# A two-layer adaptive graph network on one core: Strassen's scheme for one more softmax stage, and row statistics, norm parts and weights at other places in the written-out order

## The chip, the cores and the metric

The kernel runs on one core of one Trainium2 chip. The metric is the device time of one execution in microseconds (us), smaller is better. Times of several executions of a kernel are compared by their median. All arithmetic on TensorE is float32.

## The reference

Two layers of the same form follow each other; each is an adaptive graph convolution with a residual connection and a layer norm. With N = 2048 nodes, B = 8 batches, C = 64 features and an embedding of D = 16 numbers a node:

```
layer 0:  supports I, A, 2 A A - I
layer 1:  supports I, A, 2 A A - I, S     S = softmax(relu(E E^T), axis=1)
x_g = einsum("knm,bmc->bnkc", supports, x)
w   = einsum("nd,dkio->nkio", E, weights_pool)      weights of each node
out = einsum("bnki,nkio->bno", x_g, w) + E @ bias_pool
x   = layernorm(x + out)
```

A is 2048 x 2048. So for every node block the kernel needs u = A x, then A u, in layer 1 also S x, and for every node its own 64 x 64 weights for each support.

## The kernel before

**Stages.** The work is cut into 40 stages, listed as `stages` (line 744): five phases of eight node blocks of 256 nodes each, stage n = 8 i + j. Phase A0 makes u = A x of layer 0, B0 makes A u and closes layer 0 with the norm, A1 makes u = A x of layer 1, Z1 makes S x, V1 makes A u of layer 1 and closes with the norm. So stages 16 to 23 are A1, 24 to 31 are Z1, and 32 to 39 are V1. x and u (2048 x 512) stay on chip.

**The products.** Each stage has a generator `product` that yields its matmuls one by one. A plain stage (`straight`, or `turned`) multiplies directly: in `turned` the features are held as the stationary side in 128 columns and the adjacency or softmax block of 256 nodes is streamed, which makes 64 matmuls of 128x256 into accumulators called pz. The other stages use Strassen's scheme with its Winograd sums (`strassen`, line 471): seven products (p1, p4, p7, p2, p6, p5, p3 in this order) of half-size quarters, and additions on VectorE (DVE) with temporaries (`temps`) afterwards, which also write the results to u or to the turned features t. In phases B0 and V1 the quarters and sums of A come ready from HBM; in A0 four quarters are streamed and their sums are made in place by `sum_of_a`.

**Softmax stages.** Numerators are exp(relu(E E^T) - c), c being the row maximum (S is needed transposed, E E^T is symmetric, so c and the reciprocal of the row sum are laid along the streamed nodes and broadcast over the partitions by `load_e`, which also loads the embedding of the block into e, two buffers `e2` in turn). In stages 24 and 25 `scores` makes two slices of 128 rows at a time: two matmuls (ps), one scalar_tensor_tensor on DVE (p<-ps,c 128x512) and one exponential on ScalarE (ACT), into four buffers of tag `f2k`; the division by the row sum happens on the way from pz to t (`turned_half`). From stage 26 the blocks are taken in pairs, "wide": `numerators` makes four slices at a time (128x1024) into quarters in `w_room`, the room of the node weights, which is free then; `normalize` multiplies a quarter (128x2048) by the row's reciprocal sum, and Strassen's scheme runs over two blocks, 7 products of 32 matmuls of 256 columns in stages n and n+1 together.

**Row statistics.** In A1, `scores_of_rows` makes rows of E E^T (pr) and their maximum, `statistics` the exponentials with their row sums on ACT, and `store_c` writes both to HBM for Z1.

**Other jobs of a stage.** `weights` (line 319) makes the weights of a block: groups of matmuls pw<-e,wst into the three large PSUM buffers (`ps_big`, two banks each), whose contents go to w by ACT and, every third one, by DVE; `turn` transposes x or u through PSUM (pt) and copies it to t, half by DVE and half by ACT; `apply` multiplies the features of each node by its weights (po) and adds the 4x4 diagonal blocks to acc on DVE with a mask; `post` is the layer norm in parts 0 (mean, subtraction, squares on ACT), 1 (variance, square root on ACT) and 2 (reciprocal, product, store). The large PSUM buffers serve pw, pt, ps, pr, pb and po alike. Two accumulators (`ps_acc`) serve the products.

**Order.** All engines keep the order in which the program issues their instructions (`Pinned`, line 33; this is why nearly every profile line says L43). That order is written by hand: `put(n, place, job)` and `spread` lay jobs at places 0 to 64 of stage n (scaled by the stage's `length`), and the main loop calls `catch_up` after each matmul, which issues the jobs whose place is reached. Weights of stage n are made in stage n+1 for phases A0, B0 and A1, except for the last block of B0. The adjacency comes through the queue `adj`, an `Ahead` of four stream buffers "a" (128x1024): a load is issued as soon as a buffer can be had in the order of the list `adj.order`.

```
def put(n, i, f, *args):
    plans[n].setdefault(i * stages[n].length / 64, []).append((f, args))
```

Of the kernel before, what the change touches and what calls it, by code (L numbers as in the profile page):

```python
# [48 lines left out]
def two_graph_layers(ctx: ExitStack, tc: tile.TileContext, x, x_t, adj_b, adj_q, layers, out):  # L49
# [167 lines left out]
        for q in range(4):  # L217
            pool.dma_start(out=s1[q * D:(q + 1) * D, :].bitcast(F32), in_=estk[1][(q // 2) * D:(q // 2 + 1) * D, :])

    plain = {("A0", 0), ("A0", 1), ("B0", 0), ("A1", 0)}  # L220

    factors = {1: (("quarter", (0, 0)), "A11", "B11"), 2: (("quarter", (0, 1)), "A12", "B21"), 3: (("sum", 3), "A12", "B22"),
               4: (("quarter", (1, 1)), "A22", "T4"), 5: (("sum", 0), "A21", "T1"), 6: (("sum", 1), "A22", "T2"),
# [22 lines left out]
    def load_adj(t, key):  # L246
# [6 lines left out]
        else:  # L253
# [2 lines left out]

    quarters = [("quarter", at) for at in ((0, 0), (1, 1), (1, 0), (0, 1))]
    adj = Ahead(4, lambda: stream.tile([P, 4 * NB], F32, tag="a", name="a"), load_adj,
                [key for phase in ("A0", "B0", "A1", "V1") for j in range(NBLK)
                 for key in ([("plain", j, i) for i in range(NJ // 4)] if (phase, j) in plain  # L260
                             else [(kind, j, i) for kind, i in (quarters if phase == "A0" else
                                                           [factors[p][0] for p in orders.get((phase, j), usual)])])])
    wst = Ahead(3, lambda: three.tile([P, 8, P], F32R, tag="wst", name="wst"),
                lambda t, kc: sp.dma_start(out=t.bitcast(F32), in_=wd[kc[0]][kc[1]]),
                [(k, c) for k in ((0, 0), (0, 1), (1, 0), (1, 1)) for _ in range(NBLK)
# [2 lines left out]
    class Stage:  # L268
        def __init__(self, n, phase, j):
            self.n, self.phase, self.j = n, phase, j  # L270
            self.li, self.kk = int(phase[1]), int(phase[0] != "A")
            self.half = phase == "B0"
            self.plain = (phase, j) in plain
            self.wide = phase == "Z1" and j >= 2
            self.length = 64 if self.plain or phase == "Z1" and j < 2 else 56
            self.units = C // 2 if self.half else C
            self.e2 = e2[n % 2]
            self.t = self.sq = None
            self.dev = {}


        def load_e(self):
            cols = slice(self.j * NB, (self.j + 1) * NB)
            for h in range(2):
                pool.dma_start(out=self.e2[64 * h:64 * h + 64, :].bitcast(F32), in_=estk[self.li][:, cols])
            if self.phase == "Z1":
                self.c = (one.tile([P, 2, NB], F32, tag="wsplit", name="c") if self.j == 1
                          else two.tile([P, 2, NB], F32, tag="c", name="c"))
                pool.dma_start(out=self.c, in_=cd[self.j].rearrange("k s p -> k (s p)").partition_broadcast(P))

# [130 lines left out]
        def product(self):  # L421
            if self.wide:
                if self.j % 2 == 0:
                    self.rest = self.pair[1].rest = self.strassen(X)
                    return islice(self.rest, self.length)
                return self.rest
            if self.phase == "Z1":
                return self.turned(X, self.softmax())
            if self.kk:
                return self.turned(U, self.loaded()) if self.plain else self.strassen(U)  # L430
            if self.n == 0 or (self.phase, self.j) == ("A0", NBLK - 1):
                self.slabs = U[SB * self.j:SB * self.j + SB]
            else:
                made = one.tile([P, SB, BC], F32, tag="wraw", name="u")
                self.slabs = [made[:, s, :] for s in range(SB)]
            return self.straight(X) if self.plain else self.strassen(X)
# [34 lines left out]
        def strassen(self, right):  # L471
# [8 lines left out]
            if self.wide:  # L480
                temps = [four.tile([P, BC], F32, tag="f2k", name="temp") for _ in range(3)]
                mine = {f"A{h + 1}{t + 1}": self.pair[h].quarters[t] for h in range(2) for t in range(2)}
            else:
                room = one.tile([P, 4, half], F32, tag="wsplit", name="temps")
                temps = [room[:, i, :] for i in range(4)]
                mine = {}
            nodes = NB if self.wide else P
            streamed = self.phase == "A0"
            inside = streamed or self.wide

            def quarter(name):
                if streamed:
# [24 lines left out]
            def add(dst, a, b, op=ALU.add):  # L517

                if not isinstance(dst, tuple):
                    dve.tensor_tensor(dst, a, b, op=op)  # L520
                elif self.kk == 0:
                    dve.tensor_tensor(self.slabs[dst[0]][:, dst[1] * half:(dst[1] + 1) * half], a, b, op=op)
                else:
                    if self.wide:
                        to = self.pair[dst[0]].features()[64:128, :, :]
                    else:
                        to = self.features()[0:64, dst[0] * P:(dst[0] + 1) * P, :]
                    for par in range(2):
                        of = lambda x: x[64 * par:64 * par + 64, :].rearrange("p (q n) -> p n q", n=nodes)
                        dve.tensor_tensor(to[:, :, 4 * dst[1] + par:4 * dst[1] + par + 3:2], of(a), of(b), op=op)  # L530
# [58 lines left out]
        def repeat(self, s):  # L589

            if self.wide:
                self.pair[s].store_z()
            if self.half:
                t = self.t[:, s * P:(s + 1) * P, :]
                if self.j == NBLK - 1:
                    act.copy(t[64:128, :, :], t[0:64, :, :])
                else:
                    pool.dma_start(out=t[64:128, :, :], in_=t[0:64, :, :])
# [64 lines left out]
        def numerators(self, t, part):  # L663

            ps = big("ps").rearrange("p a (m n) -> p (a m) n", n=NB)
            for i in range(4):
                m = 2 * (4 * part + i) + t
                pe.matmul(ps[:, i, :], s1[:, m * P:(m + 1) * P], self.e2, start=True, stop=True)
            p = self.quarters[t][:, part * 1024:(part + 1) * 1024]
            dve.scalar_tensor_tensor(p.rearrange("p (m n) -> p m n", n=NB), ps, 0.0,  # L670
                                     self.c[:, 0, None, :].to_broadcast([P, 4, NB]), op0=ALU.max, op1=ALU.subtract)
            act.activation(p, p, AF.Exp)

        def normalize(self, t):
            p = self.quarters[t].rearrange("p (m n) -> p m n", n=NB)
            dve.tensor_tensor(p, p, self.c[:, 1, None, :].to_broadcast([P, NJ // 2, NB]), op=ALU.mult)

# [117 lines left out]
    for n, st in enumerate(stages):  # L795
# [12 lines left out]
        elif phase == "B0":  # L808
            for c in range(NJ // 4 if st.j == 0 else 0):
                put(n, (10, 26, 36, 57)[c], st.sums_of_a, c)  # L810
            if st.j == 7:
                spread(n, 38, 54, weights)
                bursts, posts = (0, 0, 6, 10), ()
                put(n + 1, 16, st.load_x, range(SB))
                for k in range(6):
# [3 lines left out]
                bursts, posts = (19, 19, 29, 29), (38, 46.5, 50)  # L819
                put(n + 2, 5, st.load_x, range(SB))  # L820
        elif phase == "A1":
            spread(n + 1, 12, 34.5, weights)
            turned, bursts, posts = 4, (43, 43, 43, 43), (56,)
            for s, h, place in ((0, 0, 38), (0, 1, 40), (1, 0, 57), (1, 1, 60)):
                put(*((n, place) if st.j or s == 0 else (n + 1, place - 43)), st.scores_of_rows, s, h)
            put(n, 41, st.statistics, 0)
            put(*((n, 62) if st.j else (n + 1, 19)), st.statistics, 1)
            put(n + 1, 24, st.store_c)
        elif phase == "V1":
            spread(n, (22 if 0 < st.j < 7 else 12 if st.j else 4), (62 if st.j < 7 else 42), weights)  # L830
            bursts, posts = (4, 4, 4, 4), (15, 19, 23)
            put(n, 20, st.load_z)
# [6 lines left out]
                put(n + 1, place, st.post, k)  # L839
        if n + 1 < len(stages):  # L840
            if n < 25 or n > 30:
                put(n, 44 if n < 23 else 37 if n < 25 else 4, stages[n + 1].load_e)
        if phase[0] == "A":
            put(n, 48 if n == 0 else 36 if st.li == 0 else 38.5, st.bias)
            if st.li == 0:
# [2 lines left out]
                put(n, 47 if st.j else 57, st.turn, 0, "x")  # L848
        if phase != "Z1":
            put(*((1, 26) if n == 0 else (n, 54) if st.kk == 0 else (n, 30)), st.load_acc)  # L850
        elif st.wide:
            first, even, odd = (n - 2, (16, 24, 32), (40, 48, 56)) if n % 2 == 0 else (n - 2, (28, 36, 44), (4, 12, 20))
            load = ((25, 40) if n == 28 else (n - 3, 4)) if n % 2 == 0 else (n - 3, 8)
            if n == 26:
                first, even, odd, load = 25, (4, 10, 18), (20, 26, 34), (24, 40)
            elif n == 27:
                first, even, odd, load = 25, (56, 61, 67), (42, 48, 54), (25, 33)
            put(*load, st.load_e)
            for t, places in enumerate((even, odd)):
                for i, place in enumerate(places):  # L860
# [2 lines left out]
        else:  # L863
            st.p = [None] * 8
            for c in range(8):
                if c < 3:
                    put(n - 1, (50, 54, 62)[c] if n < 26 else 40 + 8 * c, st.scores, c)
                else:
                    put(n, 8 * (c - 3), st.scores, c)

    last = stages[-1]
    for c in (2, 3):
        put(len(stages) - 1, 50, last.apply, c)
    for part, place in enumerate((58, 61)):
        put(len(stages) - 1, place, last.post, part, 8, 16)
    for n, st in enumerate(stages):
        done = 0
        todo = sorted(plans[n])
# [9 lines left out]
            catch_up()  # L888
        done = 1000
        catch_up()  # L890
    last.post(2, 8, 16)
    last.apply(0)
    last.post(0, 0, 4)
    last.apply(1)
    for part, g0, g1 in ((1, 0, 4), (0, 4, 8), (2, 0, 4), (1, 4, 8), (2, 4, 8)):
        last.post(part, g0, g1)


# [44 lines left out]
```

## Time and profile before

| what | us |
|---|---|
| median of three executions | 1470.1 |
| their range | 1469.12 to 5120.87 |
| the profiled execution | 1468.38 |
| its span in the profile | 1466.6 |
| TensorE (PE) busy | 1443.3 |
| DVE busy | 962.8 |
| ACT busy | 478.1 |
| product 1 of stage 17 starts | 623.54 |
| first matmul pz of stage 24 starts | 919.77 |
| product 1 of stage 26 starts | 996.18 |

The longest of the three times, 5120.87, stands alone, so the median and the lowest are the ones to compare with. The profile is of one execution: its span is from the first to the last instruction. A row of the timeline gives start, duration, engine, line, operation, out<-in, shape, count and in brackets the idle time of that engine just before with what ended it. Rows of one group in a row are merged, so that "x12" can span more than one matmul, and a float32 matmul appears as two rows (float32r ones as one).

### The profile page before, as it was taken

To read this page: it belongs to the slowest core of one execution; us is meant where nothing else is said; L and a number is where in the kernel's file an instruction comes from. 1 tells how busy PE (TensorE), PEld (TensorE's weight loads), DVE (VectorE), ACT (ScalarE), POOL (GpSimd) and SP (SyncE) were. 2 spreads that over 40 slices of the span, in tenths; PEclk is the share of its full clock that TensorE was granted. 3 is DMA by queue.
4 is the path that set the end of the run, shared out by engine and by line. 5 is a ranking of instruction groups with operands and counts; after the bars stand their busy time and mean duration, and the time that the engine had idled before them with its cause. 6 is when DMAs were issued, how large, how long until landed. Compare 5 with 4: busy or idle time off the path is not lost.

```text
span 1466.6 us, 31370 instructions
## 1 busy us (share of the span) xinstructions
PE 1443.3 (98%) x13406; PEld 1184.7 (81%) x13406; DVE 962.8 (66%) x1638; ACT 478.1 (33%) x595; POOL 204.4 (14%) x339
## 2 busy tenths in 40 slices
PE   9999999999999999999999999999999999999996
PEld 4577777778999998568777777788888988888885
DVE  3866666648676766865666666568794666666666
ACT  1444444432211213154444344422110233333332
POOL 5212221110111111111011111111000000000000
PEclk9999999999999999999999999999999999999999
DMA  9888888886666666589787877311313766666662
GB/s 362 275 261 276 283 281 265 282 313 193 206 192 205 206 206 193 161 172 194 196 198 169 205 210 190 77 51 58 90 43 107 252 195 192 189 193 190 191 200 62
DMA packets 88379, 285.49 MB, mean 195 GB/s; under 512 B 14000, under 2 KB 19632, under 8 KB 86640
## 3 DMA queue, kind: packets, MB, share of 16 engines
q1 hardware_dynamic: 55568, 175.13, 40.9%
q0 software_dynamic: 27200, 94.71, 21.3%
q10 hardware_dynamic: 5472, 13.63, 2.8%
q8 instruction: 106, 1.74, 0.5%
q14 instruction: 33, 0.27, 0.1%
HBM read 217.33 MB, written 62.41 MB: 191 GB/s over the span
## 4 chain that ended last, share of the span: by engine, by line
PE 93%; DVE 3%; DMA 2%; issue 1%; ACT 1%; ACTq 0%; DVEq 0%
PE p L43 57%; PE po L43 14%; PE pw L43 9%; PE pz L43 6%; PE pu L43 4%; PE pt L43 1%; DMA wst<-wd 1%; PE ps L43 1%; PE pr L43 1%; DVE acc L43 1%; DVE u L43 1%; DMA x<-in_x 1%; DVE mean L43 0%; ACT w L43 0%; DVE t L43 0%
## 5 line engine op out<-in xcount | busy, mean ns | idle before, releaser
L43 ACT ACTIVATE w<-pw 128x1024 f32<-128x1024 f32 x330 | 320.0, 1022 | 431.6 <-PE pw L43 429.9
L43 DVE SCALAR_TENSOR_TENSOR acc<-po,mask,acc 128x256 f32<-128x256 f32 (+1 forms) x640 | 247.1, 427 | 72.8 <-PE po L43 62.5
L43 DVE COPY w<-pw 128x1024 f32<-128x1024 f32 x118 | 144.4, 1224 | 140.9 <-PE pw L43 140.6
L43 PE MATMUL p<-a,u 128*128 128x128 f32 x1920 | 233.7, 278 | 0.8 <-issue 0.8
L43 PEld LDWEIGHTS p<-a,u 128*128 128x128 f32 x1920 | 221.1, 192 | 8.9 <-issue 2.7
L43 PE MATMUL po<-w,t 128*32 128x256 f32 (+1 forms) x5120 | 206.5, 337 | 6.7 <-issue 5.1
L43 PE MATMUL p<-u,a 128*128 128x256 f32 x832 | 204.3, 388 | 0.0
L43 PEld LDWEIGHTS po<-w,t 128*32 128x32 f32 (+1 forms) x5120 | 128.2, 108 | 78.7 <-issue 15.5
L43 PEld LDWEIGHTS p<-u,a 128*128 128x128 f32 x832 | 151.6, 190 | 29.2 <-issue 5.4
L43 PE MATMUL p<-x,a 128*128 128x256 f32 x624 | 152.4, 384 | 0.0
L43 PE MATMUL pw<-e,wst 64*128 64x256 f32 x1728 | 147.0, 297 | 3.1 <-DMA wst<-wd 1.2
L43 PEld LDWEIGHTS pw<-e,wst 64*128 64x128 f32 x1728 | 112.5, 184 | 45.3 <-issue 21.2
L43 PEld LDWEIGHTS p<-x,a 128*128 128x128 f32 x624 | 114.7, 190 | 19.3 <-issue 0.5
L43 PE MATMUL p<-a,x 128*128 128x128 f32 x768 | 93.0, 277 | 0.0
L43 PEld LDWEIGHTS p<-a,x 128*128 128x128 f32 x768 | 88.3, 192 | 2.4
L43 PE MATMUL pu<-x,a 128*128 128x512 f32 x192 | 87.4, 603 | 1.0 <-DMA x<-in_x 1.0
L43 PE MATMUL p<-w,u 128*128 128x256 f32 x384 | 85.8, 379 | 0.0
L43 PE MATMUL p<-a,w 128*128 128x128 f32 x672 | 81.6, 277 | 0.0
L43 PEld LDWEIGHTS p<-w,u 128*128 128x128 f32 x384 | 72.1, 190 | 9.3
L43 PEld LDWEIGHTS p<-a,w 128*128 128x128 f32 x672 | 77.4, 192 | 2.6 <-issue 1.4
L43 PEld LDWEIGHTS pu<-x,a 128*128 128x128 f32 x192 | 35.3, 191 | 41.7 <-issue 37.6
L43 ACT ACTIVATE sq<-acc 128x1024 f32<-128x1024 f32 (+2 forms) x19 | 17.5, 923 | 157.8 <-DVE acc L43 145.3
(123 smaller groups left out, 1392.4 us busy)
## 6 DMA issues: line engine op xcount, KB each, us to landing
wst<-wd SPq DMA_DIRECT2D x108, 512.0 KB, 6.5
a<-in_adj_q SPq DMA_DIRECT2D x90, 512.0 KB, 5.5
a<-sd SPq DMA_DIRECT2D x88, 512.0 KB, 4.7
sd<-a POOLq DMA_DIRECT2D x24, 512.0 KB, 6.4
bx<-bx POOLq DMA_DIRECT2D x32, 256.0 KB, 5.6
acc<-bx POOLq DMA_DIRECT2D x16, 512.0 KB, 7.2
pd<-acc POOLq DMA_DIRECT2D x16, 512.0 KB, 4.5
acc<-pd POOLq DMA_DIRECT2D x16, 512.0 KB, 8.6
```

The costliest lines, as they stand in the source:

```text
L43: return self._tc.keep_in_program_order(f(*args, **kwargs))
```

## The change

Stage 25 (softmax, j=1), called `narrow`, no longer goes through `turned` but through `strassen`: seven products of 16 matmuls of 128 columns. Its numerators are kept in four of the adjacency's stream buffers, taken by `take_halves` at place 1 of stage 24, are made in two groups of four slices for each of the two row parities, and are normalised before the product (`normalize`); the sums of the quarters are made in place on DVE. Its c lies in the room `wraw` rather than `wsplit`, since Strassen's temporaries take that, and `load_e` for it moves from place 37 to place 26 of stage 24. The adjacency's queue ends with phase A1, and V1's loads are appended at place 10 of stage 26. The numerators and normalisations of stages 26 and 27 move by a few places.

Apart from that stage: the weights of A1 j=7 (made in stage 24) go from places 12 to 34.5 to places 4 to 24, those of A1 j=0 (made in stage 17) to 14 to 36, those of B0 j=7 from place 38 to place 35 at their start. `statistics` of the first half of A1 j=0 goes from place 41 of stage 16 to place 7 of stage 17, behind the turn of u at place 4. At the end, `post` part 1 of the second half of the last stage goes behind the product, and two of the last norm parts change order.

The diff, without what only passes names on:

```diff
@@ -217,7 +217,7 @@
-    plain = {("A0", 0), ("A0", 1), ("B0", 0), ("A1", 0)}
+    plain = {("A0", 0), ("A0", 1), ("B0", 0), ("A1", 0), ("Z1", 0)}
@@ -256,10 +256,15 @@
     adj = Ahead(4, lambda: stream.tile([P, 4 * NB], F32, tag="a", name="a"), load_adj,
-                [key for phase in ("A0", "B0", "A1", "V1") for j in range(NBLK)
+                [key for phase in ("A0", "B0", "A1") for j in range(NBLK)
                  for key in ([("plain", j, i) for i in range(NJ // 4)] if (phase, j) in plain
                              else [(kind, j, i) for kind, i in (quarters if phase == "A0" else
-                                                           [factors[p][0] for p in orders.get((phase, j), usual)])])])
+                                                           [factors[p][0] for p in usual])])])
+
+    def load_last_phase():
+        adj.order += [(kind, j, i) for j in range(NBLK) for kind, i in (factors[p][0] for p in orders.get(("V1", j), usual))]
+        adj.fill()
+
     wst = Ahead(3, lambda: three.tile([P, 8, P], F32R, tag="wst", name="wst"),
@@ -272,7 +277,8 @@
             self.wide = phase == "Z1" and j >= 2
-            self.length = 64 if self.plain or phase == "Z1" and j < 2 else 56
+            self.narrow = phase == "Z1" and j == 1
+            self.length = 64 if self.plain else 56
             self.units = C // 2 if self.half else C
@@ -284,7 +290,7 @@
             if self.phase == "Z1":
-                self.c = (one.tile([P, 2, NB], F32, tag="wsplit", name="c") if self.j == 1
+                self.c = (one.tile([P, 2, NB], F32, tag="wraw", name="c") if self.j == 1
                           else two.tile([P, 2, NB], F32, tag="c", name="c"))
@@ -424,6 +430,8 @@
                 return self.rest
+            if self.narrow:
+                return self.strassen(X)
             if self.phase == "Z1":
@@ -483,10 +491,10 @@
                 temps = [room[:, i, :] for i in range(4)]
-                mine = {}
+                mine = {f"A{h + 1}{t + 1}": self.halves[h, t] for h in range(2) for t in range(2)} if self.narrow else {}
             nodes = NB if self.wide else P
             streamed = self.phase == "A0"
-            inside = streamed or self.wide
+            inside = streamed or self.wide or self.narrow
@@ -524,7 +532,8 @@
                     else:
-                        to = self.features()[0:64, dst[0] * P:(dst[0] + 1) * P, :]
+                        r = 64 if self.narrow else 0
+                        to = self.features()[r:r + 64, dst[0] * P:(dst[0] + 1) * P, :]
                     for par in range(2):
@@ -590,6 +599,8 @@
                 self.pair[s].store_z()
+            if self.narrow and s == 0:
+                self.store_z()
             if self.half:
@@ -666,12 +677,30 @@
                 pe.matmul(ps[:, i, :], s1[:, m * P:(m + 1) * P], self.e2, start=True, stop=True)
+            if self.narrow:
+                for h in range(2):
+                    at = slice(h * P, h * P + P)
+                    p = self.halves[h, t][:, part * 512:(part + 1) * 512]
+                    dve.scalar_tensor_tensor(p.rearrange("p (m n) -> p m n", n=P), ps[:, :, at], 0.0,
+                                             self.c[:, 0, None, at].to_broadcast([P, 4, P]), op0=ALU.max,
+                                             op1=ALU.subtract)
+                    act.activation(p, p, AF.Exp)
+                return
             p = self.quarters[t][:, part * 1024:(part + 1) * 1024]
...
+        def take_halves(self):
+            self.halves = {(h, t): stream.tile([P, 4 * NB], F32, tag="a", name="p") for h in range(2) for t in range(2)}
+
         def normalize(self, t):
+            if self.narrow:
+                for h in range(2):
+                    p = self.halves[h, t].rearrange("p (m n) -> p m n", n=P)
+                    dve.tensor_tensor(p, p, self.c[:, 1, None, h * P:h * P + P].to_broadcast([P, NJ // 2, P]),
+                                      op=ALU.mult)
+                return
             p = self.quarters[t].rearrange("p (m n) -> p m n", n=NB)
@@ -809,7 +838,7 @@
             if st.j == 7:
-                spread(n, 38, 54, weights)
+                spread(n, 35, 54, weights)
                 bursts, posts = (0, 0, 6, 10), ()
@@ -819,11 +848,11 @@
         elif phase == "A1":
-            spread(n + 1, 12, 34.5, weights)
+            spread(n + 1, *((4, 24) if st.j == 7 else (12, 34.5) if st.j else (14, 36)), weights)
             turned, bursts, posts = 4, (43, 43, 43, 43), (56,)
...
                 put(*((n, place) if st.j or s == 0 else (n + 1, place - 43)), st.scores_of_rows, s, h)
-            put(n, 41, st.statistics, 0)
+            put(*((n, 41) if st.j else (n + 1, 7)), st.statistics, 0)
             put(*((n, 62) if st.j else (n + 1, 19)), st.statistics, 1)
@@ -839,7 +868,7 @@
             if n < 25 or n > 30:
-                put(n, 44 if n < 23 else 37 if n < 25 else 4, stages[n + 1].load_e)
+                put(n, 44 if n < 23 else 37 if n < 24 else 26 if n < 25 else 4, stages[n + 1].load_e)
         if phase[0] == "A":
@@ -848,13 +877,19 @@
             put(*((1, 26) if n == 0 else (n, 54) if st.kk == 0 else (n, 30)), st.load_acc)
+        elif st.narrow:
+            put(24, 1, st.take_halves)
+            for t, places in enumerate(((30, 35, 39), (41, 56, 60))):
+                for i, place in enumerate(places):
+                    put(24, place, *((st.numerators, t, i) if i < 2 else (st.normalize, t)))
+            put(26, 10, load_last_phase)
         elif st.wide:
...
             if n == 26:
-                first, even, odd, load = 25, (4, 10, 18), (20, 26, 34), (24, 40)
+                first, even, odd, load = 25, (4, 12, 18), (22, 30, 36), (24, 40)
             elif n == 27:
-                first, even, odd, load = 25, (56, 61, 67), (42, 48, 54), (25, 33)
+                first, even, odd, load = 25, (66, 69, 72), (44, 52, 58), (25, 8)
             put(*load, st.load_e)
@@ -864,15 +899,14 @@
                 if c < 3:
-                    put(n - 1, (50, 54, 62)[c] if n < 26 else 40 + 8 * c, st.scores, c)
+                    put(n - 1, (50, 54, 62)[c], st.scores, c)
                 else:
...
         put(len(stages) - 1, 50, last.apply, c)
-    for part, place in enumerate((58, 61)):
-        put(len(stages) - 1, place, last.post, part, 8, 16)
+    put(len(stages) - 1, 58, last.post, 0, 8, 16)
     for n, st in enumerate(stages):
@@ -888,11 +922,12 @@
         catch_up()
+    last.post(1, 8, 16)
     last.post(2, 8, 16)
...
     last.apply(1)
-    for part, g0, g1 in ((1, 0, 4), (0, 4, 8), (2, 0, 4), (1, 4, 8), (2, 4, 8)):
+    for part, g0, g1 in ((0, 4, 8), (1, 0, 4), (2, 0, 4), (1, 4, 8), (2, 4, 8)):
         last.post(part, g0, g1)
```

## The prediction

> **What bounds the kernel now.** I read the busy shares and the chain of waits first, then TensorE's list of waits, then the instruction groups by shape, then the timeline of stages 17, 24 to 26 and the tail. The page:
>
> ```profile
> PE 1443.3 (98%) x13406; PEld 1184.7 (81%) x13406; DVE 962.8 (66%) x1638; ACT 478.1 (33%) x595; POOL 204.4 (14%) x339
> ...
> PE 93%; DVE 3%; DMA 2%; issue 1%; ACT 1%; ACTq 0%; DVEq 0%
> ```
>
> TensorE (PE) is the bound: every microsecond of matmul saved is one of span, unless PE then waits. The list of PE's waits shows how few it has (columns: total us, times, longest):
>
> ```profile
> PE po L43 <- DVE t L43: 1.6, 1, 1.6
> PE pw L43 <- DMA wst<-wd: 1.2, 2, 0.7
> PE pw L43 <- ACT w L43: 1.1, 3, 0.4
> ...
> PE pt L43 <- ACT u L43: 1.0, 1, 1.0
> ```
>
> So a better order can win at most a few us, and each place that now fits is one where a new wait can appear. Prices, from the groups by shape (busy us, mean ns):
>
> ```profile
> L43 PE MATMUL p<-a,u 128*128 128x128 f32 x1920 | 233.7, 278 | 0.8 <-issue 0.8
> ...
> L43 PE MATMUL pz<-p,x 128*128 128x256 f32 x256 | 60.7, 382 | 0.0
> ```
>
> A float32 matmul leaves two rows. Start to start the rows are 0.112 us apart at 128 columns and 0.216 at 256, so 0.224 and 0.432 us a matmul.
>
> Stage 24 (softmax, j=0) shows what the change moves:
>
> ```profile
> 921.50 1.04 PE L43 MATMUL pt<-ident,u 128*128 128x128 f32 x8
> ...
> 926.16 1.25 PE L43 MATMUL pw<-e,wst 64*128 64x256 f32 x12
> ...
> 926.93 1.23 DVE L43 COPY w<-pw 128x1024 f32<-128x1024 f32 x1
> ...
> 927.60 1.94 ACT L43 ACTIVATE w<-pw 128x1024 f32<-128x1024 f32 x2
> ...
> 943.36 1.08 POOL L43 DMA_DIRECT2D e<-ed  x2 [7.07 <-PE pw L43]
> ```
>
> The turn (pt) runs before the first weights (pw), each pw group takes all three big PSUM buffers, and their copies take 1.23 us on DVE or about 1.0 on ACT. The embedding loads for stages 25 and 26 wait for the last pw, because it reads the buffer that the first of them overwrites.
>
> [...] (the pt wait of 1.0 above is for an ACT copy queued behind two exponentials). [...] the trace has more for the embedding loads, and that is used:
>
> ```profile
> DMA to landing us min/median/max: 2.5/3.8/4.8
> ```
>
> [...] 2.29 us for 128x2048 against 1.22 for 128x1024. So two half-size operations cost what one costs plus about 0.15 us.
>
> **The change part by part** (all against the profiled execution of 1468.38 us, span 1466.6; the median of the runs shown is 1470.1, so 1.7 is added at the end at most).
>
> *Work.* Stage 25 has 64 matmuls of 256 columns, 64 x 0.432 = 27.65 us. Strassen's 7 products of 16 at 128 columns are 112 x 0.224 = 25.09. That is -2.56. Its scores go from eight pairs of matmuls to four groups of four, the same 16 matmuls, +0.1 or so. Work: -2.4. The rest is whether PE can be fed.
>
> *Stages 24 and 25: five new waits.* I followed PE's new order with these durations.
> (1) The first pw group, now at place 4, takes the three big buffers just before pt(u). pt must have the first one back. It is DVE's copy, which starts at about 922.5 and ends 1.23 later at 923.7; PE arrives at 922.6. Wait 1.15.
> (2) The next pw group comes four matmuls after the turn, and its third buffer is that of pt, whose last copy on DVE follows two on ACT (0.63 each). It ends at about 928.0, PE is there 0.9 earlier.
> (3) The scores that follow need the buffer of the weights copy behind it on ACT: 0.7.
> (4) The last pw ends at about 940.8. The load of the embedding for stage 25, at place 26 rather than 37, can issue only then (941.1 and 941.65), and the first numerators at place 30 need it. With the median landing of 3.8 it is there at 945.4, and PE is there at 943.6: 1.9. With 2.5 it is 0.6, with 4.8 it is 2.9. Before, a plain stage's own scores needed this load only 13 us later, so nothing showed.
> (5) At the end of stage 24 the DVE has in its queue, behind the last scores of stage 25's odd half: two STT of 0.69, two normalisations of 1.22 and the two t of the last pz. Product 1 of stage 25 needs the first normalised quarter and the PSUM of pz, and is held 2.0.
> Sum 6.7, less 0.3 of waits on ACT there that go: +6.4. Stage 25 itself keeps DVE busy for about 27.4 of its 28.4 us (STT 7.3, sums of A 4.9, normalisations 6.9, temps 2.5, t 3.4, t from pz 2.8), and products 5 and 3 arrive with a margin near 0. I take no wait there. If two or three products wait 0.4 to 1, that is +0 to +3, kept for the range. With the work of -2.4, product 4 of stage 26, now at 1003.57, starts at about 1007.6: **+4.0**. PE runs in order, so each of these waits holds every matmul behind it and is paid in full; behind the waiting loads on GpSimd's queue stand only the norm parts c, stage 26's loads and a store of acc, none of them due within 8 us.
>
> *Statistics of A1 j=0 behind the turn of stage 17.* Meant is that the exponentials no longer stand before ACT's t and u copies. Before:
>
> ```profile
> 624.50 1.25 ACT L43 ACTIVATE t<-pt 64x512 f32<-64x512 f32 x2
> 625.77 0.60 ACT L43 ACTIVATE u<-pu 128x512 f32<-128x512 f32 x1
> 626.42 1.09 PE L43 MATMUL pt<-ident,u 128*128 128x128 f32 x8 [1.00 <-ACT u L43]
> ```
>
> But ACT's t copies share a tile with DVE's (622.96, 1.42 long), and wait for them, to 624.4. So the u copy moves by 0.2 only, pt with it. The exponentials (3.7 us with table load and accumulator reads) now stand at about 630.4 to 634.2, before the copies of the first weights on ACT; and the weights, from 14 to 36, now come after five matmuls of the product, with the row scores (pr) right behind them. pr needs a buffer from DVE's w copy, which stands behind a sum of 2.29 us. That is 1.9 of wait, then 0.1 on the second pr and 0.35 and 0.7 on pw behind ACT. In all some 3.9 (of which 0.8 is the part of the pt wait that stays), against 2.4 before: **+1.4**, between 0.9 and 1.5.
>
> *Weights of B0 j=7 from place 35.* Two waits of pw on ACT (0.30 and 0.41) go. What is late next is DVE's and ACT's t before po, now at 589.43; they are done at about 588.75: **-0.7**. At worst 0.
>
> *Tail.* The deviations' reduction moves behind t, so po, which waits 1.57 for it at 1453.32, starts about 0.6 earlier. The new order of the last norm parts has one deviation wait on ACT behind the other half's square, about +0.5. **-0.1**, bounds -0.6 and +0.4.
>
> *At nothing.* The queue of V1's adjacency loads: the stream buffers come free at about 999 and stage 32 starts about 1148; stages 26 to 31 hide it, and if they did not it would cost one landing of about 5 us. Sums of A in place, c in another room, the moved loads on SP and POOL: SP has no other load there, POOL waits only for what is told in (4). The numerators of stages 26 and 27: four groups shift by 2 to 10 places inside stages whose DVE load is counted above.
>
> Sum +4.0 +1.4 -0.7 -0.1 = +4.6: profiled about 1473.0, median 1474.7 at most; I say 1474.5.
>
> **Rivals.**
> (A) *Releases and landings come before PE needs them.* For it: the five waits are differences of 0.7 to 2.0 us between times that each carry half a microsecond of error; a landing of 2.5 takes 1.3 off (4) alone. Against: (1) and (2) follow from order, not luck. With all of (1) to (5) gone the sum is -6.7 from +4.6, so -2.1, that is 1468.0. The change is faster than before once the five together are under 2.1 us, with the other parts as above.
> (B) *DVE becomes the bound of stages 25 and 26.* For it: 27.4 of 28.4 us. Against: DVE is 66% over the span, and PSUM has two accumulators. Four late hand-overs of about 1 us added to the sum give +8.6, 1478.6. It decides where DVE's work in stage 25 passes the stage's 28.4 us of PE.
> (C) *The statistics do what they are meant to.* No pt wait and no pr wait in stage 17, -0.9 in place of +1.4: +2.3, 1472.4. For it: the pt wait is real. Against: the shared tile.
>
> **Numbers.** Forecast (+3 to +7) 0.58; A 0.20; B 0.12; C 0.10. The range runs from A to B with the median's own scatter of 1 us: 1467.0 to 1478.6, written 1478.5. Two per cent, 29 us, is about what a measurement of this kernel can tell from no change; no case here reaches it. Only an unforeseen stall per stage would, which gives slower 0.02, faster 0.01, within 0.97. Small as it is, I expect the sign to be plus.
>
> **What would show it.** In the profile after: PE's waits grow by about 5 to 6 us, with pt on DVE's w, ps on the embedding load, and p of stage 25 on DVE's t or on a normalised quarter, each between 920 and 972; stage 25's pz rows turn to p rows of 128 columns; pr waits on DVE's w at about 633; po of stage 16 starts about 588.8. The forecast is wrong if ps never waits for the embedding and product 1 of stage 25 starts before 966, or if DVE is idle under 0.5 us in stage 25 with PE waiting on it more than three times.

## The result and the profile after

The changed kernel takes 1480.63 us in the median of six executions (1476.47 to 1484.54), the kernel before 1469.09 beside it. The ratio is 1.0082, with a 95% interval of 1.0059 to 1.0104: some 12 us more, between 8.7 and 15.3. The forecast of 1474.5 with a range up to 1478.5 had the sign and missed the size. The profiled execution of the changed kernel took 1478.77, its span is 1476.9.

The page of the changed kernel, busy shares and chain of waits:

```profile
PE 1444.0 (98%) x13502; PEld 1186.9 (80%) x13502; DVE 973.9 (66%) x1655; ACT 478.5 (32%) x597; POOL 204.3 (14%) x339
...
PE 90%; DVE 3%; DMA 3%; issue 2%; ACT 1%; POOL 0%; ACTq 0%; DVEq 0%; POOLq 0%
```

PE's busy time has not fallen, although 2.4 us of matmul work went, and its share of the chain has dropped from 93% to 90%. A busy time that doesn't fall with the work is the first sign that some matmuls ran slower. PE's waits (columns: total us, times, longest):

```profile
PE ps L43 <- DMA e<-ed: 5.1, 1, 5.1
PE po L43 <- issue: 4.6, 8, 1.0
PE p L43 <- DVE t L43: 1.9, 1, 1.9
PE pr L43 <- DVE w L43: 1.8, 1, 1.8
PE pw L43 <- DMA wst<-wd: 1.7, 3, 0.8
PE pt L43 <- DVE w L43: 1.1, 1, 1.1
PE pw L43 <- DVE t L43: 1.1, 1, 1.1
...
PE po L43 <- DVE t L43: 0.9, 1, 0.9
PE pt L43 <- ACT u L43: 0.8, 1, 0.8
PE ps L43 <- ACT w L43: 0.7, 1, 0.7
```

All five waits of stages 24 and 25 that the prediction named are there, four of them within 0.2 us of their size: 1.1 (1.15 forecast), 1.1 (0.9), 0.7 (0.7), 1.9 (2.0). So are the wait of pr on DVE (1.8 against 1.9) and the part of pt's wait that stays (0.8). The fifth, for the embedding, is 5.1 and not 1.9. Timeline of stage 24 there (start, duration, and in brackets the idle time before):

```profile
941.14 0.73 POOL L43 DMA_DIRECT2D cd<-inv  x1 [19.52 <-issue]
...
941.96 1.08 POOL L43 DMA_DIRECT2D e<-ed  x2
...
949.82 1.12 PE L43 MATMUL ps<-e,s 128*128 128x256 f32 x4 [5.13 <-DMA e<-ed]
950.74 1.91 PE L43 MATMUL pz<-p,x 128*128 128x256 f32 x4
```

Two things stand in these four lines. Ahead of the embedding loads on GpSimd's queue, 0.8 us earlier, goes the store cd<-inv, the row statistics of the last block. And after the wait four pz rows take 1.91 us, where in the kernel before eight take 1.89 (at 919.77). Transfers issued in that stretch (KB each, median us to landing):

```profile
c<-cd POOLq DMA_DIRECT2D x1, 256.0 KB, 6.4
e<-ed POOLq DMA_DIRECT2D x2, 64.0 KB, 7.4
cd<-inv POOLq DMA_DIRECT2D x1, 1.0 KB, 8.1
```

The store is 1 KB, 256 values of four bytes, two from each of the 128 partitions, and lands at 941.14 + 8.1 = 949.2. The first half of the embedding lands at 941.96 + 7.5 = 949.5, just behind it. Busy time by stretch (the column before the last two is the clock granted to TensorE, as a share of full speed; the last two are the busy share of the DMA engines and the GB/s that they moved):

```profile
944.00:949.00 5.00, 0.69 (x4) 0.26 (x2) 0.00 (x0) 0.00 (x0) 0.04 (x1) 1.00 0.19 61
...
946.50:949.80 3.30, 0.00 (x0) 0.01 (x1) 0.00 (x0) 0.00 (x0) 0.00 (x0) 1.00 0.00 0
...
949.00:951.00 2.00, 1.18 (x5) 1.21 (x6) 0.02 (x1) 0.00 (x0) 0.00 (x0) 0.73 0.00 0
951.00:953.00 2.00, 2.00 (x7) 1.64 (x7) 1.27 (x2) 1.23 (x2) 0.00 (x0) 0.50 0.00 0
953.00:955.00 2.00, 2.00 (x12) 1.78 (x11) 0.69 (x1) 0.63 (x1) 1.61 (x3) 0.92 0.07 18
...
633.00:634.00 1.00, 1.00 (x4) 0.82 (x3) 0.80 (x2) 1.00 (x2) 0.00 (x0) 0.50 0.00 0
```

In the last 3.3 us of the wait, from 946.5 to 949.8, the DMA engines moved nothing at all. So the bytes of the embedding were through by 946.5, and the trace has the landing of the first half 3.0 us later, at 949.5. What lies between the two is not shown.

The clock was at 0.50 from 949.9 to 953.3, and once more from 632.5 to 635.9, behind the wait of pr in stage 17:

```profile
631.72 0.73 PE L43 MATMUL pr<-s,e 128*128 128x512 f32 x2 [1.82 <-DVE w L43]
```

That is twice 3.413 us. Matmuls take twice as long there, as the pz rows show (four in 1.91 us, eight in 1.89 before), so half of 3.413, an estimated 1.7 us, is lost each time where PE has work throughout. In the kernel before the clock stays at 1.00 from 5.3 us until the tail, at 1459.4.

The forecast's landmarks in the traces, as stretches between two matmuls, so that the scatter of the stages ahead drops out:

| stretch | before | after | forecast of the difference |
|---|---|---|---|
| a po of stage 15 (567.2 before) to pt of x in stage 17 | 52.9 | 51.5 | -0.7 |
| pt of x in stage 17 to that in stage 18 | 40.96 | 43.76 | +1.4 |
| first pz of stage 24 to product 4 of stage 26 | 83.80 | 93.19 | +4.0 |

The two spans differ by 10.3 only, because the first two stages, which the change does not touch, ran 1.8 us faster in the second profile (the turn in stage 2 at 93.88 against 95.69).

### The profile page after: what moved, and what is told of

It is laid out like the page before. It is cut to its first block, busy times and chain, and to the rows that moved or that the text cites. A ratio compares the mean times of both kernels' runs of the same rounds, so it can differ in the third digit from the quotient of the medians.

```text
span 1476.9 us, 31604 instructions
## 1 busy us (share of the span) xinstructions
PE 1444.0 (98%) x13502; PEld 1186.9 (80%) x13502; DVE 973.9 (66%) x1655; ACT 478.5 (32%) x597; POOL 204.3 (14%) x339
## 4 chain that ended last, share of the span: by engine, by line
PE 90%; DVE 3%; DMA 3%; issue 2%; ACT 1%; POOL 0%; ACTq 0%; DVEq 0%; POOLq 0%
PE p L43 58%; PE po L43 14%; PE pw L43 8%; PE pu L43 4%; PE pz L43 3%; DMA wst<-wd 2%; PE pt L43 1%; PE ps L43 1%; PE pr L43 1%; DVE acc L43 1%; DVE u L43 1%; DMA x<-in_x 1%; DMA e<-ed 0%; DVE t L43 0%; DVE mean L43 0%
## 5 line engine op out<-in xcount | busy, mean ns | idle before, releaser
L43 DVE TENSOR_TENSOR temps<-p,temps 128x256 f32<-128x256 f32 x115 | 45.8, 419 | 33.6 <-PE p L43 32.7
```

Source lines behind the costliest of these rows:

```text
L43: return self._tc.keep_in_program_order(f(*args, **kwargs))
```

## The experiments

**The store moved behind the load (store_c_late).**

```diff
-            put(n + 1, 24, st.store_c)
+            put(n + 1, 34 if st.j == 7 else 24, st.store_c)
```

> The changed kernel with one edit: the store of the last row statistics (cd of block 7) goes from place 24 to place 34 of stage 24, behind the embedding load for stage 25 on GpSimd's queue. Theory [...]: the load lands 2.5 to 4.8 us after its issue instead of 7.4, PE's wait for it falls from 5.1 to between 0.6 and 2.9 us, the half clock behind it goes [...], and the median falls from 1480.6 by 3 to 6.5 us. Rival (the queue had been idle and its first transfer is slow, or the load itself is slow): the wait stays at about 5 us and the time does not move.

1474.54 us, ratio to before 1.0045 (1.0028 to 1.0062), so 5.4 us less than the changed kernel. Here and below such a difference is taken from the two ratios to the kernel before, which was measured again beside each set of runs. Its timeline:

```profile
942.55 1.05 POOL L43 DMA_DIRECT2D e<-ed  x2 [28.21 <-PE pw L43]
...
945.69 0.71 PE L43 MATMUL ps<-e,s 128*128 128x256 f32 x4 [0.41 <-DMA e<-ed]
...
950.38 0.73 POOL L43 DMA_DIRECT2D cd<-inv  x1 [5.21 <-DVE p L43]
951.10 1.08 POOL L43 DMA_DIRECT2D e<-ed  x2
```

The load, first on a queue that had been idle for 28 us, landed after 2.5 us, and PE waited 0.4 instead of 5.1 (0.6 to 2.9 were expected). That rules out the rival of the idle queue. The next load, for stage 26, now stands behind the store, and it took 7.1:

```profile
e<-ed POOLq DMA_DIRECT2D x2, 64.0 KB, 7.1
```

So the delay goes with the place behind the store: 2.5 us ahead of it, 7.1 behind it. Why, the runs do not show; in the changed kernel the bytes of the load were through 3.3 us before PE went on. Behind the short wait the matmuls run at full speed: four pz rows take 1.03 us, against 1.91 behind the long one. (In this execution a half-clock stretch stood behind product 1 of stage 25 instead, from 973.0; its mean granted clock is 0.997, that of e_own_room 0.998.)

**The embedding in its own room (e_own_room).**

```diff
             cols = slice(self.j * NB, (self.j + 1) * NB)
+            if self.narrow:
+                self.e2 = one.tile([P, NB], F32R, tag="row", name="e2")
...
-                put(n, 44 if n < 23 else 37 if n < 24 else 26 if n < 25 else 4, stages[n + 1].load_e)
+                put(n, 44 if n < 23 else 37 if n < 24 else 10 if n < 25 else 4, stages[n + 1].load_e)
```

> The changed kernel with stage 25's embedding in a room of its own (tag row), loaded at place 10 of stage 24, so that neither the load nor the scores wait for the last weights. Theory: PE's wait of 5.1 us for the load and the 3.4 us at half clock behind it both go, 5.1 + 1.7 = 6.8 us, median about 1473.8. Rival (what is lost there is a matter of DVE or of PSUM, and the wait only shows it first): another wait of several us takes its place and less than 3 us is won.

1472.76 us, ratio 1.0032 (1.0019 to 1.0044): 7.3 us less than the changed kernel (6.8 were expected). The wait for the embedding is gone, nothing takes its place, and no stretch before the tail is at half clock (mean granted clock 0.998, as in the kernel before). From pz to product 4 of stage 26 it takes 86.21 us, 2.4 over before, where the prediction without its wait (4) gives 4.0 - 1.9 = 2.1.

**Stages 16 and 17 as before (stage17_back).**

```diff
-            spread(n + 1, *((4, 24) if st.j == 7 else (12, 34.5) if st.j else (14, 36)), weights)
+            spread(n + 1, *((4, 24) if st.j == 7 else (12, 34.5)), weights)
...
-            put(*((n, 41) if st.j else (n + 1, 7)), st.statistics, 0)
+            put(n, 41, st.statistics, 0)
```

> The changed kernel with stages 16 and 17 as before: statistics of the first half of A1 j=0 at place 41 of stage 16 and the weights in stage 17 from place 12 to 34.5. Theory (the new order costs 1.4 us of waits and 1.7 us for 3.4 us at half clock): 3.0 us are won, median about 1477.6, and the trace shows full clock through stage 17. Rival (the half clock came by chance and is not tied to the wait): 1.4 us are won and a half-clock stretch of 3.4 us stands there or elsewhere.

1477.22 us, ratio 1.0068 (1.0053 to 1.0083). The gain of some 2 us lies between the two expectations, and the intervals overlap, so the time alone decides nothing. The trace does: from pt in stage 17 to pt in stage 18 it takes 40.92 us (40.96 before), at full clock (1.00 from 625 to 640). In store_c_late and e_own_room, which keep the new order, it takes 42.05 and 42.04 without a half-clock stretch, against 43.76 with one. So the new order costs 1.1 us in all three profiles that have it, and 1.7 more in one of them.

**Stalls of chosen length in the kernel before (stalls).** Ten calls of this, at place 10 of stages 28 to 31 and place 1 of stages 33 to 38:

```diff
+    def stall(k):
+        ps = big("px")
+        pe.matmul(ps[:, 0, 0:P], ident, ident, start=True, stop=True)
+        scratch = one.tile([P, P], F32, tag="row", name="scratch")
+        act.activation(scratch, ps[:, 0, 0:P], AF.Copy)
+        for _ in range(k):
+            act.activation(scratch, scratch, AF.Copy)
+        ps = big("py")
+        pe.matmul(ps[:, 0, 0:P], scratch, scratch, start=True, stop=True)
```

> The kernel before with ten stalls put into TensorE's stream, in stages 28 to 31 and 33 to 38: a small matmul, a chain of 2 to 11 copies of 128x128 on ScalarE, and a matmul that needs the last copy. From the copies of 128x256 (0.37 us) a chain makes PE wait some 0.9 to 4 us. It leaves nothing of the work out. Theory 1 [...]: only stalls of 3.4 us and more are followed by 3.4 us at clock 0.5. Theory 2 [...]: stalls from about 1.8 us up are followed by it, those between 1.8 and 3.4 in part, those under 1.7 never. Each costs 1.7 us on top of the stall.

It took 1500.61 us in one execution. Four of its stalls, in order of time:

```profile
1111.31 0.49 PE L43 MATMUL py<-scratch 128*128 128x128 f32 x2 [2.46 <-ACT scratch L43]
1232.03 0.49 PE L43 MATMUL py<-scratch 128*128 128x128 f32 x2 [2.14 <-ACT scratch L43]
1275.32 0.49 PE L43 MATMUL py<-scratch 128*128 128x128 f32 x2 [2.82 <-ACT scratch L43]
1400.74 0.80 PE L43 MATMUL py<-scratch 128*128 128x128 f32 x2 [3.84 <-ACT scratch L43]
```

The clock reads 0.50 from 1232.4 to 1235.8, from 1276.8 on (to 1280.0 at least), and from 1399.7 to 1406.4: behind the stall of 2.14, behind that of 2.82, and 1.0 us before the end of that of 3.84, where it stayed low for 6.7 us at least. Behind the one of 2.46 there is none. That refutes theory 1: stalls of 2.14 and 2.82, under 3.4, were followed by half clock. In after and in stalls the changes of clock lie whole multiples of 3.413 us apart: in after 317.4 us from 632.5 to 949.9, which is 93 times that; in stalls 44.4 from 1232.4 to 1276.8, which is 13 times, and 122.9 on to 1399.7, which is 36. The waits of PE, as the lists and timelines have them, and the clock behind each:

| kernel, wait | us | clock behind it | read from |
|---|---|---|---|
| store_c_late, ps in stage 24 | 0.41 | 1.00 | four pz rows in 1.03 us |
| stalls, at 1317.66 | 1.80 | 1.00 | clock from 1315 to 1320 |
| after, pr in stage 17 | 1.82 | 0.50 | clock from 632.5 to 635.9 |
| weights_late, product 1 of stage 25 | 1.89 | 1.00 | 14 rows in 1.80 us, as in normalise_early without a wait |
| after, product 1 of stage 25 | 1.9 | 1.00 | clock from 977.6 to 1005.5 |
| stalls, at 1232.03 | 2.14 | 0.50 | clock from 1232.4 to 1235.8 |
| stalls, at 1111.31 | 2.46 | 1.00 | seven rows of 256 columns in 1.68 us (eight pz rows in 1.89 before) |
| stalls, at 1275.32 | 2.82 | 0.50 | clock from 1276.8 to 1280.0 |
| stalls, at 1400.74 | 3.84 | 0.50 | clock from 1399.7 to 1406.4 |
| after, ps in stage 24 | 5.13 | 0.50 | clock from 949.9 to 953.3 |
| stage17_back, ps in stage 24 | 5.2 | 0.50 | ps rows up to 0.774 us, against 0.469 in store_c_late |

Of theory 2 the part on lengths holds: of the waits from 1.8 to 3.4 us some are followed by half clock and some are not, and in after those of 1.1 and less are not. Length alone does not decide: 1.82 and 2.14 were followed by it, 2.46 was not. What else decides was not shown.

**The weights of stage 24 late again (weights_late).** On top of e_own_room and stage17_back:

```diff
-            spread(n + 1, *((4, 24) if st.j == 7 else (12, 34.5)), weights)
+            spread(n + 1, 12, 34.5, weights)
```

> e_own_room with stages 16 and 17 as before and the weights in stage 24 at places 12 to 34.5 again, so that of the waits in stage 24 only the one of product 1 of stage 25 on DVE is left. Theory (waits 1 to 3 come from the weights at places 4 to 24): from the first pz of stage 24 to product 4 of stage 26 it takes 83.8 (before) - 2.4 (work) + 2.0 (the wait left) - 0.3 = 83.1 us, against 86.2 in e_own_room; with 0.8 won in B0 and, in somewhat under half of the executions, 1.7 lost to a half-clock stretch behind the last wait, the median is 0 to 1 us below that of before. Rival (the numerators at places 30 to 41 collide with the weights for the three large PSUM buffers): new waits on ACT's or DVE's w of 1 us and more there, median 1 us or more above before.

1468.42 us, ratio 0.9996 (0.9988 to 1.0004). From pz to product 4 it takes 83.29 us; 83.1 were expected. Waits (1) to (3) are gone, the one on DVE is left:

```profile
966.89 1.80 PE L43 MATMUL p<-p,x 128*128 128x128 f32 x14 [1.89 <-DVE t L43]
```

**Numerators and normalisation earlier (normalise_early).** On top of that:

```diff
-            for t, places in enumerate(((30, 35, 39), (41, 56, 60))):
+            for t, places in enumerate(((32.5, 37, 40), (41, 47, 50))):
```

> weights_late with the numerators and normalisations of stage 25 at places (32.5, 37, 40) and (41, 47, 50) instead of (30, 35, 39) and (41, 56, 60), so that DVE is through with them before the last pz. Theory (product 1 waits since the second normalisation stands ahead of the t copies on DVE): the wait of 1.9 us goes, the stretch from pz to product 4 takes 83.1 - 1.9 = 81.2 us, no half clock, the median is about 3 us below before (ratio 0.998). Rival (DVE is the bound there, the wait only moves on): product 4 or 7 of stage 25 waits about as long, and the time is that of weights_late.

1466.11 us, ratio 0.9981 (0.9973 to 0.9989), 2.8 us below before: the only one of these kernels with an interval wholly below before. From pz to product 4 it takes 81.23 us; 81.2 were expected. Here DVE is free when pz ends, and product 1 follows without a wait:

```profile
964.27 1.39 DVE L43 TENSOR_TENSOR t<-pz,c 64x512 f32<-64x512 f32 x2 [1.61 <-PE pz L43]
965.81 1.80 PE L43 MATMUL p<-p,x 128*128 128x128 f32 x14
966.00 1.39 DVE L43 TENSOR_TENSOR t<-pz,c 64x512 f32<-64x512 f32 x2 [0.33 <-PE pz L43]
```

## Why the prediction was wrong in size

**The work: right.** -2.4 was forecast, and -0.3 for short waits on ACT that go; normalise_early, with every wait of these stages gone, shows 81.23 - 83.80 = -2.57 for the two together.

**Waits (1), (2), (3) and (5): right,** by the list of waits and by weights_late and normalise_early, which take them away and win 2.9 and 2.1 us in the traces.

**Wait (4): the step that failed.** It took 3.8 us, the median landing of the embedding loads between 900 and 1010, none of which follows a store closely, and bounded it by 4.8. (That bound was narrow even for the trace of before: its embedding loads between 653 and 899, with other traffic on the DMA engines, took 5.4 to 9.2 us.) The sentence on GpSimd's queue named what stands behind the waiting loads and not what stands ahead. `store_c` is issued at place 24, the load now at 26; before, the load was at 37 and was issued 7.8 us after the store, at 943.36. The trace of before had the store and its price, in the transfers issued between 934 and 937:

```profile
935.57 0.72 POOL L43 DMA_DIRECT2D cd<-inv  x1 [14.85 <-ACT w L43]
...
cd<-inv POOLq DMA_DIRECT2D x1, 1.0 KB, 8.6
```

With 941.1 + 8.6 in place of 941.65 + 3.8 the wait comes out as 6.1; it measured 5.1. What the traces show of GpSimd's queue: in after the load's landing, at 949.5, is 0.3 us behind the store's, at 949.2, and 3.0 us after 946.5, from where on the DMA engines moved nothing; in store_c_late loads took 2.5 us ahead of the store and 7.1 behind it. This term was 3.2 us too small.

**The half clock: missing altogether.** The prediction counted a wait at its length. Where the clock stands at 0.50 for 3.413 us behind it, as in after, it costs 1.7 more by the estimate above. The wait for the embedding is followed by half clock in both profiles that have it at full length (5.1 us in after, 5.2 in stage17_back). Of the waits of 1.8 and 1.9 us (pr in stage 17, product 1 of stage 25) 2 of the 8 in the profiles are (pr in after, product 1 in store_c_late); what decides which was not shown, and I take it for chance. The changed kernel's six executions spread over 8 us, where those of the kernel before lie within 2.6 but for one. The two shorter waits can account for up to 3.4 of that; the rest stays open, as no trace of the slowest or the fastest of the six was kept.

**Stage 17: right but for the clock.** +1.4 was forecast, +1.1 is what the order costs at full clock, +2.8 with a half-clock stretch as in the profile after. The lists have waits of 1.8, 0.8 and 0.4 us in stage 17, 3.0 in all, against 1.0, 0.5 and 0.4 before, 1.9 in all. The reason given, that ACT's t copies wait for DVE's anyway, holds: pt waits 0.8 instead of 1.0.

**B0: agrees, within the scatter.** From po in stage 15 to pt in stage 17 the six kernels with the new places take 51.5 to 52.6 us, 51.9 in the mean, the two with the old ones 52.9 and 52.2: -0.7, and -0.7 was forecast. No run changes these places alone, and the two old ones differ by as much. The waits of pw on ACT fall from three to one, as the prediction has it. **Tail: right.** po's wait falls from 1.6 to 0.9, and from the last po to the end of DVE it takes 0.6 more: 0.0, -0.1 was forecast.

**The sum.** Forecast +4.6, the landing +3.2, the half clock behind it +1.7, that behind the two shorter waits 2 x 2/8 x 1.7 = +0.9, stage 17 -0.3: +10.1, of 12.0 measured with an interval from 8.7. The +0.9 is an estimate from the 2 in 8 above. In the traces about 0.5 of the rest lies in stages 24 to 26 (9.4 measured; 4.0, 3.2 and 1.7 make 8.9); where the remainder lies stays open.

**The rivals.** A fails: none of the five waits stayed away. B fails: from product 1 of stage 25 to stage 26 DVE was busy for 23.4 of 27.9 us, not 27.4 of 28.4. The parts that the prediction lists add up to 27.8, not 27.4, and about half of the t copies of the last pz, 2.8 us, lies ahead of product 1, where wait (5) had them already. Products 5 and 3 did not wait. C fails: both waits of stage 17 are there. The upper end of the range, 1478.5, has B's time without the 1 us of scatter that the lower end has; with it the range would reach 1479.6, still under the 1480.63 measured.

## What to carry to other kernels

When a load is moved up, read what stands ahead of it on its queue, not only what follows: behind a store of one kilobyte, of four-byte values, the same 64 KB landed after 6.9 to 7.6 us, ahead of it after 2.5. No run shows whether a store in longer pieces would do the same. On an engine-bound kernel, price a wait by its length and then by the clock: here waits of 1.8 us and more in PE's list could be followed by 3.413 us at clock 0.50, an estimated 1.7 more, and in after those of 1.1 were not. A scheme that saves work pays only in an order in which its new hand-overs fit; the same Strassen stage stood in a kernel 12 us slower than before and in one 2.8 us faster, and the difference is where a load and its buffer, the weights, the statistics, the numerators and the normalisations were put.

## What the runs showed of the hardware that I had not expected

Behind waits of 1.82 to 5.2 us TensorE's clock stood at 0.50, twice for 3.413 us in after; behind other waits, of 1.80, 1.89 and 2.46 us, it stayed at 1.00. In a stall of 3.84 us it fell 1.0 us before the stall was over and was still at 0.50 6.7 us later. In after and in stalls its changes lie whole multiples of 3.413 us apart (93, 13 and 36). The last store cd<-inv, 256 values of four bytes, takes 8.6 us to land in before, 8.1 in after and 7.9 in store_c_late. Embedding loads that land in 2.5 us ahead of it (store_c_late) take 6.9 to 7.6 right behind it, in after, stage17_back and store_c_late; in after the DMA engines move nothing in the last 3.3 us of PE's wait for them.
